# First attention of a two-layer block: values and ones in one product, maxima as rows of the queries, both kinds of scores interleaved over four row groups

## The chip, the cores and the metric

The kernel runs on one core of one Trainium2 chip. The metric is device time in microseconds, the median of three runs. A further execution was profiled; times of single instructions come from it. PE is the matmul engine, PEld its weight loads, DVE the vector engine, ACT the scalar (activation) engine, POOL the general SIMD engine, SP the engine whose queue issues the DMAs. SBUF is the on-chip memory, PSUM the eight banks that PE writes.

## The reference, cut to what matters

Two layers are computed one after the other. Each normalises its input, modulates it per sample, runs an attention-like part, adds the result to the input, and does the same with a feed-forward-like part. Only the first attention is touched by the change:

```python
# x: (16, 256, 128); sa, ca, ga: per-sample modulation, (16, 1, 128)
h = _layernorm(x, axis=-1) * (1 + ca) + sa
x = x + ga * _L0_attn_ref(h, Wq, bq, Wk, bk, Wv, bv, Wo, bo)

def _L0_attn_ref(hidden_states, Wq, bq, Wk, bk, Wv, bv, Wo, bo):
    HIDDEN, HEADS, HEAD_DIM = 128, 16, 8
    SCALE = HEAD_DIM ** (-0.5)
    b, s, d = hidden_states.shape
    q = (hidden_states @ Wq.T + bq).reshape(b, s, HEADS, HEAD_DIM)
    k = (hidden_states @ Wk.T + bk).reshape(b, s, HEADS, HEAD_DIM)
    v = (hidden_states @ Wv.T + bv).reshape(b, s, HEADS, HEAD_DIM)
    scores = jnp.einsum('bqhd,bkhd->bhqk', q * SCALE, k)
    probs = jax.nn.softmax(scores.astype(jnp.float32), axis=-1)
    out = jnp.einsum('bhqk,bkhd->bqhd', probs, v).reshape(b, s, d)
    return out @ Wo.T + bo
```

After it come a six-layer local transformer, a state-space layer and a low-rank linear layer. The change leaves their code as it is.

## The kernel before

`block_kernel` computes both modulations, then calls `full_attention`, `local_transformer` and `state_space`. The whole activation stays in SBUF, features on partitions (`c.xT`, 128 by 4096). `full_attention` (L132 to L425) is the first attention. Its unit of work is one sample (`u`, 16 of them, 256 tokens); two samples make a group (`g`, 8 of them). The 16 heads are numbered as four row groups `r` (32 partitions each) by four heads `j` within a row group, 8 features each.

**Per group**, `before` (a Python generator, L183) loads the tokens (`xin`), transposes them into `xT` (`px`), takes mean and variance on DVE (`a0st`, `a0mv`), the inverse root on POOL (`inv_sqrt`, L53), normalises on DVE (`xn`, L212), transposes to features (`to_features`, tile `ln`, result `hT`), and makes queries and keys. The query tile `qm` (L223) has four copies of the queries, one for each `j`; in copy `j` a per-partition scale `hm` zeroes all partitions but those of head `j`, so that 32 rows can be used where a head has only 8. Two copies are written by ACT (L226) and two by DVE (L231).

**Per sample**, `values` (L246) makes the value tile `vp`, in which each head has 8 columns of values and 32 of zeros; `turn` (L290) transposes the negated row maxima, as bfloat16 high and low parts made by POOL (L287, L288), into `nT`; `after` (L368) divides by the sums (`rT`, `oT`), multiplies by the output weights (`py`), and adds to `xT`.

**Per step** `k` (64 of them, four to a sample) three things happen. `scores(k, half)` (L263) computes scores with the queries on partitions, 128 queries of two heads `j` in the two row groups of that half, into two PSUM banks `s` (two buffers in all), and DVE takes the maxima (L283). `exponentials(k)` (L306) computes the same scores again with the keys on partitions, 128 keys by 2 heads by 256 queries, in all four row groups (L314, tile `sT`, four banks), adds the negated maxima by eight bfloat16 products with a selection matrix `selm` (L325), and ACT exponentiates (L336, tile `e`). `gather(k, j)` (L339) multiplies the exponentials by the values into `po[:, 0]` and by a tile of ones into `po[:, 1]`, in four column groups of 32 (L359); the first gather of a sample clears the bank with four bfloat16 products (`zb`, L347).

**The order** is written out by hand (`tc.manual_schedule()`, L395 to L425): every engine takes its instructions in the order in which this loop issues them. In step `k` come `exponentials(k)`, `scores(k + 5, 0)`, a slot, `gather(k - 1, 0)`, a slot, `scores(k + 5, 1)`, `gather(k - 1, 1)`, a slot. A slot runs the first pending generator up to its next `yield`. Pending ones are `before` of a later group (appended when `k % 8 == 3`), and, put in front of it, `values`, `turn` (one step before its sample's first exponentials) and `after`. So the first five steps have scores alone, and the last five exponentials and gathers alone. All of `px`, `ln`, `pq`, `pk`, `pv`, `pm`, `py` share one PSUM bank (tag `mm`, one buffer, L147): each waits until the reader of the one before it is done. In float32 every product shows as two records of PE and two weight loads.

Of the kernel before, what the change touches and what calls it, by code (L numbers as in the profile page):

```python
# [10 lines left out]
F32 = mybir.dt.float32  # L11
# [120 lines left out]
def full_attention(c, a, m):  # L132
# [4 lines left out]

    nc, tc = c.nc, c.tc
    HJ, R = 4, 32
    with ExitStack() as ctx:  # L140
# [8 lines left out]

        w4 = wp.tile([P, 4, D], F32, tag="w4", name="w4")  # L150
        for j, n in enumerate(("WqT", "WkT", "WvT", "WoT")):
            nc.sync.dma_start(w4[:, j, :], a[n])
        b3 = wp.tile([P, 3], F32, tag="b3", name="b3")
        nc.sync.dma_start(b3, a["b0"])
        bv = wp.tile([P, D], F32, tag="bv", name="bv")
        nc.sync.dma_start(bv, a["bv"].partition_broadcast(P))

        hm = wp.tile([P, HJ], F32, tag="hm", name="hm")
        nc.sync.dma_start(hm, a["c_head"])
# [3 lines left out]
        selm = wp.tile([P, HJ, P], BF16, tag="selm", name="selm")  # L163
        sel1 = wp.tile([P, HJ], F32, tag="sel1", name="sel1")
        nc.sync.dma_start(sel1, a["c_hmax"])
        nc.vector.tensor_copy(selm, sel1.unsqueeze(2).to_broadcast([P, HJ, P]))
        zb = wp.tile([P, R], BF16, tag="zb", name="zb")
        nc.gpsimd.memset(zb, 0.0)

        VB = R + HD0  # L170
        one = wp.tile([P, HJ * VB], F32, tag="one", name="one")
        nc.gpsimd.memset(one, 0.0)
        nc.gpsimd.memset(one.rearrange("p (h x) -> p h x", x=VB)[:, :, 0:HD0], 1.0)
        vp, nms = [], []
        for i in range(2):
            t = wp.tile([P, NT, H0 * VB], F32, tag=f"vp{i}", name=f"vp{i}")
            nc.gpsimd.memset(t, 0.0)
            vp.append(t)
            t = wp.tile([P, NT, HJ, R], BF16, tag=f"nm{i}", name=f"nm{i}")
            nc.gpsimd.memset(t, 0.0)  # L180
            nms.append(t)

        def before(g, q):  # L183
# [25 lines left out]
            yield  # L209
            xn = sb.tile([P, n, D], F32, tag="xn", name="xn")  # L210
            for i in range(n):
                nc.vector.tensor_scalar(  # L212
                    xn[:, i, :], xin[:, i, :], mv[:, i, 0:1], r[:, i : i + 1], ALU.subtract, ALU.mult
                )
                if i % 2:
                    yield
# [7 lines left out]
            for j in range(HJ):  # L224
                if j % 2 == 0:
                    nc.scalar.activation(  # L226
                        qm[:, :, j, :], pq, AF.Identity, bias=hb[:, j : j + 1], scale=hm[:, j : j + 1]
                    )
            for j in range(HJ):
                if j % 2:  # L230
                    nc.vector.tensor_scalar(  # L231
                        qm[:, :, j, :], pq, hm[:, j : j + 1], hb[:, j : j + 1], ALU.mult, ALU.add
                    )
            yield
            pk = ps.tile([P, GT], F32, tag="mm", name="pk")
            nc.tensor.matmul(pk, w4[:, 1, :], hTf, start=True, stop=True)
            kT = gp.tile([P, G, S], F32, tag="kT", name="kT")
            nc.scalar.activation(
                kT.rearrange("p b s -> p (b s)"), pk, AF.Identity, bias=b3[:, 1:2], scale=1.0
            )  # L240
# [3 lines left out]
        tops, rows_, sums, exps = {}, {}, {}, {}  # L244

        def values(u):  # L246
            g, b = divmod(u, G)
            v, hT = vp[b], made[g]["hT"]
            pv = ps.tile([P, NT, D], F32, tag="mm", name="pv")
            for t in range(NT):  # L250
                nc.tensor.matmul(
                    pv[:, t, :], hT[:, b, t * P : (t + 1) * P], w4[:, 2, :], start=True, stop=True
                )
            for t in range(NT):
                nc.vector.tensor_tensor(
                    v[:, t, :].rearrange("p (h x) -> p h x", x=VB)[:, :, 0:HD0],
                    pv[:, t, :].rearrange("p (h x) -> p h x", x=HD0),
                    bv.rearrange("p (h x) -> p h x", x=HD0),
                    ALU.add,
                )  # L260
            yield

        def scores(k, half):  # L263
# [5 lines left out]
            if i == 0 and half == 0:  # L269
                tops[u] = sb.tile([P, NT, HJ, HJ], F32, tag="mx", name="mx")  # L270
            ss = [sp.tile([P, 2, S], F32, tag="s", name="s") for _ in range(2)]
            for j in range(2):
                for r, s in enumerate(ss, 2 * half):
                    rows = slice(r * R, (r + 1) * R)
                    nc.tensor.matmul(  # L275
                        s[:, j, :],
                        qm[rows, b, jj + j, t * P : (t + 1) * P],
                        kT[rows, b, :],
                        start=True,
                        stop=True,  # L280
                    )
            for r, s in enumerate(ss, 2 * half):
                nc.vector.tensor_reduce(tops[u][:, t, r, jj : jj + 2], s, AX.X, ALU.max, negate=True)  # L283
            if i == 3 and half == 1:
                nm = nms[b]
                hi, lo = nm[:, :, :, 0:HJ], nm[:, :, :, HJ : 2 * HJ]
                nc.gpsimd.tensor_copy(hi, tops[u])  # L287
                nc.gpsimd.tensor_tensor(lo, tops.pop(u), hi, ALU.subtract)  # L288

        def turn(u):  # L290

            nm = nms[u % G]
            pm = ps.tile([P, NT, P], F32, tag="mm", name="pm")
            for t in range(NT):
                nc.tensor.matmul(
                    pm[:, t, :],
                    nm[:, t].rearrange("p r x -> p (r x)"),
                    c.identb,
# [3 lines left out]
            rows_[u] = sb.tile([P, S], BF16, tag="nT", name="nT")  # L302
            nc.vector.tensor_copy(rows_[u], pm.rearrange("p t x -> p (t x)"))
            yield

        def exponentials(k):  # L306
            u, i = divmod(k, 4)
            g, b = divmod(u, G)
            jj, kt = 2 * (i // 2), i % 2
            qm, kT, nT = made[g]["qm"], made[g]["kT"], rows_[u]  # L310
            ss = [tp.tile([P, 2, S], F32, tag="sT", name="sT") for _ in range(HJ)]
            for r, s in enumerate(ss):
                rows = slice(r * R, (r + 1) * R)
                nc.tensor.matmul(  # L314
                    s,
                    kT[rows, b, kt * P : (kt + 1) * P],
                    qm[rows, b, jj : jj + 2, :],
                    start=True,
                    stop=True,
                    skip_group_check=True,  # L320
                )
            for j in range(2):
                for r, s in enumerate(ss):
                    rows = slice(r * R, (r + 1) * R)
                    nc.tensor.matmul(  # L325
                        s[:, j, :],
                        selm[rows, jj + j, :],
                        nT[rows, :],
                        start=False,
                        stop=True,  # L330
                        skip_group_check=True,
                    )
            exps[k] = []
            for s in ss:
# [1122 lines left out]
```

## Time and profile before

| what | value |
| --- | --- |
| median of 3 runs | 4379.85 us (4375.7 to 4380.5) |
| the profiled execution: time, span | 4380.97 us, 4379.2 us (so 1.8 us lie outside the span) |
| busy over the span: PE, PEld, DVE, ACT, POOL | 95%, 57%, 80%, 57%, 58% |
| first scores (L275) start | 29.0 us |
| first exponentials' products (L314) start | about 63 us |
| last step with scores ends | 438.0 us |
| last gather ends | about 458.7 us |
| two samples in the middle, one group made beside them (224.53 to 276.03) | 51.50 us: PE 49.23, DVE 31.17, ACT 20.15, POOL 3.39 busy |
| one sample near the end, no group made (379.03 to 402.52) | 23.49 us: PE 23.30, DVE 13.57, ACT 8.26, POOL 1.18 busy |

How to read it: the first attention is the stretch from about 17 us, where its weights are loaded, to about 463 us, some 10% of the span. In the views quoted below a row of the table by stages gives, after the stretch and its length, each engine's busy time and instruction count, then the clock that PE was granted (1.00 is full speed, 0.50 half), the share of the DMA engines and GB/s. A row of the timeline gives start, duration, engine, line, operation, tiles written and read, shapes, how many instructions were merged, and in brackets how long the engine sat idle before and for whom. A busy PE is not PE at its peak: its records overlap, so the distance from one start to the next tells more than a duration.

### The profile page before, as it was taken

How to read it: one execution, taken by the hardware profiler on the slowest of the kernel's cores; microseconds unless marked ns; L12 is line 12 of the kernel's file. 1: busy time of each engine (PE TensorE's matmuls, PEld its weight loads, DVE VectorE, ACT ScalarE, POOL GpSimd, SP SyncE). 2: the span in 40 equal slices, each digit the busy share in tenths (PEclk: the TensorE clock that was granted, in tenths of full speed). 3: DMA queues.
4: the chain of work that ended last, by engine and by line, in shares of the span. 5: the costliest groups of instructions: out<-in, count | busy, mean ns of one | idle time of the engine just before them, and what ended most of it. 6: DMA issues, size and time to landing. Idle time of an engine off the chain costs nothing. (4 is left out here: it accounts for less than half of the span.)

```text
span 4379.2 us, 100775 instructions
## 1 busy us (share of the span) xinstructions
PE 4146.0 (95%) x43950; PEld 2479.5 (57%) x43950; DVE 3521.1 (80%) x4992; ACT 2483.0 (57%) x3219; POOL 2530.8 (58%) x1532
## 2 busy tenths in 40 slices
PE   7999599999999999999999999999999999779998
PEld 4455355565665655656556565565665655445554
DVE  4665588888888888888888888888888988459997
ACT  2333455555555555555555555555555555379995
POOL 0000366656666666666666666666666666258887
PEclk9999799999999999999999999999999999889999
DMA  0000100000000000000000000000000000033433
GB/s 23 6 4 1 54 2 1 2 2 22 7 2 2 2 22 6 2 2 2 22 6 2 1 2 22 6 2 1 2 2 2 2 1 2 13 97 105 114 104 85
DMA packets 58773, 82.86 MB, mean 19 GB/s; under 512 B 5256, under 2 KB 30428, under 8 KB 57564
## 3 DMA queue, kind: packets, MB, share of 16 engines
q1 hardware_dynamic: 58332, 76.41, 6.3%
q8 instruction: 346, 5.67, 0.5%
q14 instruction: 95, 0.78, 0.1%
HBM read 73.78 MB, written 2.62 MB: 17 GB/s over the span
## 5 line engine op out<-in xcount | busy, mean ns | idle before, releaser
L594 POOL TENSOR_TENSOR u<-u,w 128x1024 f32<-128x1024 f32 x384 | 902.0, 2360 | 323.9 <-DVE w L577 183.6
L608 POOL TENSOR_TENSOR u<-u,r 128x1024 f32<-128x1024 f32 x384 | 720.3, 1902 | 176.3 <-DVE r L604 176.3
L561 ACT ACTIVATE sq<-pq 128x1024 f32<-128x1024 f32 x384 | 388.5, 1024 | 665.1 <-PE pq L554 331.1
L554 PE MATMUL pq<-wqk,F 128*128 128x512 f32 x1536 | 723.0, 598 | 4.0 <-ACT sq L561 1.4
L694 POOL TENSOR_TENSOR pp<-pp,sm 128x1024 f32<-128x1024 f32 x192 | 367.1, 1912 | 619.9 <-DVE sm L690 619.9
L731 PE MATMUL py<-at,wvo 128*128 128x256 f32 x3072 | 714.4, 383 | 2.3 <-ACT at L722 2.3
L712 PE MATMUL pa<-pT,xw 32*128 32x512 f32 x3072 | 653.4, 617 | 30.3 <-ACT sq L561 29.3
L731 PEld LDWEIGHTS py<-at,wvo 128*128 128x128 f32 x3072 | 570.4, 191 | 134.9 <-issue 47.9
L566 DVE TENSOR_TENSOR u<-pq,cosl 128x1024 f32<-128x1024 f32 x384 | 463.3, 1207 | 190.4 <-ACT sq L561 190.4
L577 DVE TENSOR_TENSOR w<-pq,sinl 128x512 f32<-128x512 f32 x768 | 491.3, 681 | 82.9 <-PE pq L554 82.5
L722 ACT COPY at<-pa 128x1024 f32<-128x1024 f32 x384 | 383.6, 1012 | 277.0 <-PE pa L712 274.1
L588 DVE TENSOR_REDUCE ss<-sq 128x16 f32<-128x1024 f32 x384 | 455.8, 1198 | 2.6 <-ACT sq L561 1.1
L554 PEld LDWEIGHTS pq<-wqk,F 128*128 128x128 f32 x1536 | 273.8, 191 | 275.7 <-issue 244.1
L617 PEld LDWEIGHTS pt<-ident,u 128*128 128x128 f32 x3072 | 350.0, 142 | 123.9 <-issue 73.2
L617 PE MATMUL pt<-ident,u 128*128 128x128 f32 x3072 | 400.0, 276 | 20.0 <-POOL u L608 19.6
L712 PEld LDWEIGHTS pa<-pT,xw 32*128 32x128 f32 x3072 | 234.1, 185 | 291.2 <-issue 182.7
L1219 DVE TENSOR_TENSOR_SCAN s<-da,db 128x512 f32<-128x512 f32 x256 | 301.4, 1208 | 25.8 <-PE db L1213 11.5
L795 PE MATMUL fp<-hT,w 128*128 128x512 f32 (+1 forms) x576 | 268.0, 602 | 39.8 <-DVE w L577 38.0
L657 PEld LDWEIGHTS s<-kT,qT 64*32 64x32 f32 x24576 | 254.4, 105 | 82.0 <-issue 81.0
L283 DVE TENSOR_REDUCE mx<-s 128x2 f32<-128x512 f32 x256 | 164.8, 686 | 152.2 <-PE s L275 150.3
L657 PE MATMUL s<-kT,qT 64*32 64x64 f32 x24576 | 285.5, 226 | 0.5 <-ACT kT L625 0.5
L1229 PE MATMUL y<-hc,ident 128*128 128x512 f32 x512 | 244.3, 604 | 16.0 <-POOL hc L1223 14.2
(214 smaller groups left out, 6199.5 us busy)
## 6 DMA issues: line engine op xcount, KB each, us to landing
btd<-bc SPq DMA_DIRECT2D x72, 512.0 KB, 5.3
bte<-bc SPq DMA_DIRECT2D x56, 256.0 KB, 5.2
wqk<-in_Wqk SPq DMA_DIRECT2D x6, 1024.0 KB, 7.8
wv<-in_LWvT SPq DMA_DIRECT2D x6, 512.0 KB, 5.3
wo<-in_Wo SPq DMA_DIRECT2D x6, 512.0 KB, 9.0
xin<-in_x SPq DMA_DIRECT2D x8, 256.0 KB, 2.9
out<-ot SPq DMA_DIRECT2D x8, 256.0 KB, 6.2
w<-in_W SPq DMA_DIRECT2D x6, 341.0 KB, 2.9
```

The costliest lines, as they stand in the source:

```text
L554: nc.tensor.matmul(q.p[:, x], self.F[:, g.b0 + b, o : o + P], g.l.wqk[:, k, x, :], start=True, stop=True)
L561: self.c.nc.scalar.activation(q.sq, q.p, AF.Square)
L566: self.c.nc.vector.tensor_tensor(q.u.rearrange("p h x d -> p x h d"), q.p, g.l.cosl[:, t, k].unsqueeze(2).to_broadcast([P, 2, HEADS, DH // ...
L577: self.c.nc.vector.tensor_tensor(q.w[:, :, x], q.p[:, 1 - x], g.l.sinl[:, t, k, x, :].unsqueeze(1).to_broadcast([P, HEADS, DH // 2]), ALU. ...
L588: self.c.nc.vector.tensor_reduce(g.ss[b][:, t, k, :], q.sq.rearrange("p x h d -> p h x d"), AX.XY, ALU.add)
L594: self.c.nc.gpsimd.tensor_tensor(q.u, q.u, q.w, ALU.add)
L608: self.c.nc.gpsimd.tensor_tensor(uf, uf, g.r[b][:, t, k, :].unsqueeze(2).to_broadcast([P, HEADS, DH]), ALU.mult)
L617: self.c.nc.tensor.transpose(q.pt[:, j, :], uf[:, j * P : (j + 1) * P], self.c.ident)
L657: nc.tensor.matmul(s[qs, e, j, :], qT[es, j, qs], kT[es, j, ks : ks + 2 * W], start=False, stop=True, skip_group_check=True,)
L712: self.c.nc.tensor.matmul(pa[:, x, :], g.xw[b, t][qs, k, :], g.pT[b, t][qs, k, :], start=(k == 0), stop=(k == 1),)
L722: self.c.nc.scalar.copy(self.at[:, :, o : o + 2 * W].rearrange("p h (w q) -> p w h q", q=W), g.pa[b, t, i].rearrange("p w (h q) -> p w h q ...
L731: self.c.nc.tensor.matmul(g.py[b], g.l.wvo[:, h, :], self.at[:, h, :], start=(h == 0), stop=(h == HEADS - 1),)
```

## The change

Six things are done at once in `full_attention`.

1. The maxima are no longer added by separate products. They are turned in float32 (`pm`, 16 partitions), copied by ACT, and written by four DMAs per sample (one for each `j`) into a partition of each row group of `qm` that copy `j` leaves at zero (`TOP`: 24, 25, 0, 1). The keys get a second version with ones on those partitions (`kT[:, v]`, two ACT instructions per group instead of one).
2. Each head's values and ones lie side by side in `vp`, so that one product yields both output and sum; heads `j` 0 and 1 write `po[:, 0]`, heads 2 and 3 `po[:, 1]`. In `after`, `swap` products bring each sum beside its output (`pr`), and the output product is two with halved weights (`wo`). The value bias moves into the output bias (`bo`, `bg`).
3. `pair(k, h)` interleaves: two row groups compute the scores of step `k + 6`, the other two the transposed scores of step `k`, in the order first head `j` of the scores, exponents, second head `j`.
4. Work changes engines: `xn` from DVE to POOL, `vp`, `nT`, `yg` from DVE to ACT, one of four `qm` copies from DVE to ACT, the division from DVE to POOL, with a new copy `o` of the sums by ACT before it.
5. `AHEAD` goes from 5 to 6; `before` starts at `k % 8 == 2`, `turn` at `k % 4 == 2`, ahead of `values`; the `yield`s move.
6. The loads at the start are in another order, with four new constants.

```diff
-        def exponentials(k):
+        def exponents(k, h):
+            u, i = divmod(k, 4)
+            g, b = divmod(u, G)
+            jj, kt = 2 * (i // 2), i % 2
+            qm, kT = made[g]["qm"], made[g]["kT"]
+            ss = []
+            for r in range(2 * h, 2 * h + 2):
+                rows = slice(r * R, (r + 1) * R)
+                s = tp.tile([P, 2, S], F32, tag="sT", name="sT")
+                nc.tensor.matmul(s, kT[rows, jj // 2, b, kt * P : (kt + 1) * P],
+                    qm[rows, b, jj : jj + 2, :], start=True, stop=True)
+                ss.append((r, s))
+            return ss
+        def exponentials(k, ss):
+            for r, s in ss:
+                e = pp.tile([P, 2, S], F32, tag="e", name="e")
+                nc.scalar.activation(e, s, AF.Exp)
+                exps[k, r] = e
+        def pair(k, h):
+            first, second = k + AHEAD < N, 0 <= k < N
+            if first:
+                scores(k + AHEAD, h, 0)
+            if second:
+                ss = exponents(k, 1 - h)
+            if first:
+                scores(k + AHEAD, h, 1)
+                maxima(k + AHEAD, h)
+            if second:
+                exponentials(k, ss)
         def turn(u):
-            nm = nms[u % G]
-            pm = ps.tile([P, NT, P], F32, tag="mm", name="pm")
...
-            rows_[u] = sb.tile([P, S], BF16, tag="nT", name="nT")
-            nc.vector.tensor_copy(rows_[u], pm.rearrange("p t x -> p (t x)"))
+            top = tops.pop(u)
+            pm = ps.tile([HJ * HJ, NT, P], F32, tag="mm", name="pm")
+            for t in range(NT):
+                nc.tensor.matmul(pm[:, t, :], top[:, t].rearrange("p j r -> p (j r)"), c.ident, ...)
+            nT = sb.tile([HJ * HJ, S], F32, tag="nT", name="nT")
+            nc.scalar.copy(nT, pm.rearrange("p t x -> p (t x)"))
+            rows = made[g]["qm"].rearrange("(r x) b j s -> x r b j s", x=R)
+            for j in range(HJ):
+                nc.sync.dma_start(rows[TOP[j]][:, b, j, :], nT[j * HJ : (j + 1) * HJ, :])
         def gather(k, j):
-            for x in range(2):
-                for r, e in enumerate(exps[k]):
-                    w = vp[b][:, kt, o : o + R] if x == 0 else one[...]
-                    nc.tensor.matmul(sums[u][r * R : (r + 1) * R, x, :], w, e[:, j, :], ...)
+            for r in range(HJ):
+                nc.tensor.matmul(sums[u][r * R : (r + 1) * R, jj // 2, :],
+                    vp[b][:, kt * HJ + r, (jj + j) * R : (jj + j + 1) * R], exps[k, r][:, j, :], ...)
         def after(u):
-            nc.vector.reciprocal(rT, po[:, 1, :])
-            nc.vector.tensor_tensor(oT, po[:, 0, :], rT, ALU.mult)
-            yield
-            nc.tensor.matmul(py, w4[:, 3, :], oT, start=True, stop=True)
-            nc.vector.tensor_scalar(yg, py, b3[:, 2:3], m[:, 2, u : u + 1], ALU.add, ALU.mult)
+            o = sb.tile([P, 2, S], F32, tag="o", name="o")
+            nc.scalar.copy(o, sums.pop(u))
+            yield
+            for x in range(2):
+                nc.tensor.matmul(pr, swap[:, x, :], o[:, x, :], start=(x == 0), stop=(x == 1))
+            nc.vector.reciprocal(rT, pr)
+            nc.gpsimd.tensor_tensor(o, o, rT.unsqueeze(1).to_broadcast([P, 2, S]), ALU.mult)
+            yield
+            yield
+            for x in range(2):
+                nc.tensor.matmul(py, wo[:, x, :], o[:, x, :], start=(x == 0), stop=(x == 1))
+            nc.scalar.activation(yg, py, AF.Identity, bias=bg[:, u : u + 1], scale=m[:, 2, u : u + 1])
         def values(u):
-            for t in range(NT):
-                nc.vector.tensor_tensor(v[:, t, :]..., pv[:, t, :]..., bv..., ALU.add)
+            nc.scalar.copy(v..., pv...)
         def before(g, q):
                 nc.vector.bn_aggr(mv[:, i, :], st[:, i, :])
             inv_sqrt(c, r, r, [P, n])
-            yield
             for i in range(n):
-                nc.vector.tensor_scalar(xn[:, i, :], ...)
-                if i % 2:
-                    yield
+                nc.gpsimd.tensor_scalar(xn[:, i, :], ...)
+            yield
+            yield
             to_features(c, ps, xn, m, 0, 1, g, hT)
-        AHEAD, N = 5, 4 * B
+        AHEAD, N = 6, 4 * B
-                if k % 8 == 3 and (k // 8 + 2) * G < B:
+                if k % 8 == 2 and (k // 8 + 2) * G < B:
-                if k % 4 == 3 and 0 <= k + 1 < N:
-                    todo.insert(0, turn((k + 1) // 4))
                 if k % 4 == 2 and 0 <= k + 2 < N:
                     todo.insert(0, values((k + 2) // 4))
-                if 0 <= k < N:
-                    exponentials(k)
-                if k + AHEAD < N:
-                    scores(k + AHEAD, 0)
+                    todo.insert(0, turn((k + 2) // 4))
+                pair(k, 0)
                 slot()
                 if 0 < k <= N:
                     gather(k - 1, 0)
                 slot()
-                if k + AHEAD < N:
-                    scores(k + AHEAD, 1)
+                pair(k, 1)
                 if 0 < k <= N:
                     gather(k - 1, 1)
```

## The prediction

> **What bounds the kernel now.** I read the table by stages first, then the groups of the stage, then its timeline. Only the first attention changes, about 29 to 459 us. Two samples in mid-stage, and a late one without a group made beside it, read:
>
> ```profile
> 224.53:276.03 51.50, 49.23 (x552) 25.97 (x556) 31.17 (x60) 20.15 (x38) 3.39 (x7) 1.00 0.02 7
> 379.03:402.52 23.49, 23.30 (x272) 12.56 (x276) 13.57 (x22) 8.26 (x16) 1.18 (x3) 1.00 0.01 2
> ```
>
> PE is busy 96 to 99%. It is the bound, but a second loop lies close behind it:
>
> ```profile
> 271.43 1.03 PE L275 MATMUL s<-kT,qm 32*128 32x256 f32 x8
> ...
> 272.39 0.64 PE L359 MATMUL po<-e,vp 128*32 128x256 f32 x8
> ...
> 272.49 1.29 DVE L283 TENSOR_REDUCE mx<-s 128x2 f32<-128x512 f32 x2 [2.22 <-PE s L275]
> ...
> 273.39 1.57 PE L275 MATMUL s<-kT,qm 32*128 32x256 f32 x8
> ...
> 274.58 1.29 DVE L283 TENSOR_REDUCE mx<-s 128x2 f32<-128x512 f32 x2 [0.80 <-PE s L275]
> 274.89 0.64 PE L359 MATMUL po<-e,vp 128*32 128x256 f32 x8
> ...
> 275.89 1.14 PE L314 MATMUL sT<-qm,kT 32*128 32x512 f32 x8
> ```
>
> Starts give PE's prices: half a step's scores 0.96 (271.43 to 272.39), a gather 1.00 (274.89 to 275.89), and from the same timeline four exponents' products 0.96 and their eight bfloat16 products 0.22. A step is 0.96 + 0.22 + 2x0.96 + 2x1.00 = 5.10, a sample 20.4 and its slots 3.1.
> The loop: `s` has two banks, so scores wait for the maxima before (273.39, first bank; 273.83, second) and the maxima wait for the scores. Maxima follow maxima after **2.09** (272.49 to 274.58): 1.29 reducing, 0.80 waiting. Where both banks start together (280.12) the maxima begin 1.17 later (281.29), against 0.75 after the second bank where the first started 0.44 ahead; the loop is then 1.17 + 1.29 + 0.05 = 2.51. Neither `nT` nor exponentials slow this down: ACT idles before them, waiting for PE.
>
> **The change on PE.** The eight bfloat16 products go (0.22), gathers halve (1.00 to 0.57: half the 0.86 of stream, 0.14 of change-over kept), and the four exponents run beside the scores (0.96 saved). A pair with its change-over costs 1.07, with gather 1.64; a step 3.28 instead of 5.10. Over 59 steps that is 107 us of PE work, the most there is to win. That row groups run side by side, not in issue order, is seen where the first exponents begin:
>
> ```profile
> 62.45 1.32 PE L275 MATMUL s<-kT,qm 32*128 32x256 f32 x2
> ...
> 63.00 1.23 PE L314 MATMUL sT<-qm,kT 32*128 32x512 f32 x2
> ...
> 63.04 1.58 PE L275 MATMUL s<-kT,qm 32*128 32x256 f32 x5
> ```
>
> Five records of scores issued before the exponents start after them. [...]
>
> **But 1.64 is under 2.09: the loop of DVE becomes the bound**, two per step, 4.18. And PE's 0.45 of slack is just the head start that makes 2.09 rather than 2.51, so most slot work shows. Interval a runs from a step's first pair to its second, b to the next step. Prices from rows: `pv` 0.64, `px`, `ln` 0.6, `pq`, `pk` 1.06, `zb` 0.23, `py` and `pr` 1.06 each (0.63 for today's half, plus 0.43 of stream), exponentials end 2.28 after a pair starts (0.53 to the second pass, 0.59 for it, 0.08 to ACT, 1.08 for two).
> - k mod 4 = 2, a: `pm`, then `pv`, which needs its bank. ACT copies `nT` only behind the exponentials: 2.28 + 0.45 = 2.75, `pv` to 3.44. **3.44**; b 2.51.
> - 3 and 0: four of 2.09.
> - 1, a: `pr`, `zb`: 1.07 + 1.06 + 0.23 + 0.57 = **2.93**. b: reciprocal 1.76 from 2.35 to 4.1, POOL's multiply 1.32 (a 128x512 product at L1223) to 5.5, `py` 1.06: **3.68**.
>
> A sample is 20.9, today 23.49. A group made beside two samples adds: `px` and its late load 0.4, statistics 0.5; `pk` waits for the bank of `pq`, whose readers now are three ACT copies of 0.7 behind the exponentials (2.33 to 4.55), then runs to 5.65, +3.56 on 2.09; after it 2.51 instead of 2.09. Two samples: 46.7, today 51.50.
>
> **Unseen costs.** `pm` in float32: 0.22 (today's) to 0.64 (`pv`); I take 0.45. ACT's copy of 16x256: 0.19 (128x64, L1120) to 0.56 (128x256, L123); 0.45. The multiply: 0.95 (half of L608's 1.90) to 1.32; the upper, for equal shape. Together -14 to +5 us over 16 samples. POOL's `xn`: 0.37 (128x64, L597) to twice that, four times; two slots cover them, and uncovered each would delay `ln`. DMAs: 64 more on SP, 0.43 each to issue, 1.6 (`bc`) to 2.9 (`xin`) to land: the two needed first are in at 2.75 + 0.86 + 1.6..2.9 = 5.2..6.5, needed at 10.1 (3.44 + 2.51 + 2x2.09): hidden. Queued behind them on SP is only the next `xin`. The bf16 casts on POOL go from beside other work: nothing. `vp` and `yg` on ACT lie in its idle time; so do two `kT` copies.
>
> **Sum.** First scores at 29.0 as now (the loads' order and `pb` move this by -1 to +1.4). Before the first exponentials PE runs at half pace:
>
> ```profile
> 31.14 1.29 DVE L283 TENSOR_REDUCE mx<-s 128x2 f32<-128x512 f32 x2 [5.03 <-PE s L275]
> ...
> 31.89 2.67 PE L275 MATMUL s<-kT,qm 32*128 32x256 f32 x8 [0.78 <-DVE mx L283]
> 33.99 1.29 DVE L283 TENSOR_REDUCE mx<-s 128x2 f32<-128x512 f32 x2 [1.56 <-PE s L275]
> ```
>
> A half costs 2.85; today ten halves and 5.5 of slots make 34. Twelve make 34.2, and slots 8 (`pq` waits for `hT`, `pk` for `qm`): exponentials start at 71, today 63. 58 steps: 8.4 for the first two, 6 for the low clock at their start, 6x46.7, 2x20.9, 337 in all, to 408; today 375 for 59. The last six steps without scores: 6x3.28, 1.8 for `pv`, 3.3 for `py`, 1.2 for the last gather, 26, today 20.7. Last gather at 434, today 458.7: -25. The last sample's tail is longer by copy, `pr`, multiply and half of `py` (3 us), half covered by the next stage's normalisation, already running then: +1.5. So 4380.97 - 23.5 = 4357.5 for the profiled execution; against the median, 1.1 lower, **4357**.
>
> **Rivals.**
> 1. *The clock stays down* (slower). The granted clock is half at 464 to 504 us and full again only after dense work, and in the prologue the pace is half though PE looks busy:
>
> ```profile
> 32.00:36.00 4.00, 4.00 (x14) 2.82 (x16) 1.72 (x3) 0.36 (x1) 0.00 (x0) 1.00 0.00 2
> ```
>
> (The 1.00 is from before the first clock record; the products' pace is the measure.) Two row groups of four are in use there; full pace comes at 72 us, once all four and the gathers fill PE. [...] So what counts seems to be how much of the array works, and the change leaves PE more idle: `pk`'s stall is 1.9 us. At half pace an interval is 3.05 (pair 1.95, gather 1.05), slots 10 a sample: 34.5, against 23.4 on average. +11 a sample; from 2.1 cold samples on the gain is gone. Six would give **4423**. For it: warming today takes exponents, bfloat16 products and full gathers. Against: at half pace PE is the bound again, hence dense. Chance 0.17.
> 2. *The rows stored in `qm` hold back scores, or pairs run in order.* If scores of the group's other sample wait for the four DMAs, eight samples wait till 6.5 rather than 3.44: +25, **4382**. If a pair does not overlap as it says, nine of sixteen intervals lose their head start of 0.44: +29, **4386**. For: all are in one tile. Against: the rows at 63 us, and the parts written and read differ. Chance 0.20, a fifth of it slower by over 0.2%.
> 3. *The stalls hide.* Without the waits for ACT and POOL the a of 2 is 2.73, the b of 1 2.70, the `pk` interval 3.76: 1.7 a sample and 1.9 a group, -36, **4321**. For: ACT is idle two thirds of the time. Against: its queue is in order. Chance 0.19.
>
> **How the numbers follow.** The forecast has 0.44 (4343 to 4371 by the unseen costs and the start). Measurement tells 0.2%, about 9 us, from no change. Faster: 0.44 + 0.19 = 0.63; same: 0.16, four fifths of rival 2; slower: 0.17 + 0.04 = 0.21. The range goes from below rival 3 to the milder part of rival 1, two cold samples over no gain: 4315 to 4400.
>
> **What would show it.** Maxima 2.09 to 2.5 apart with DVE, not PE, behind the waits; PE under 85% busy; waits of `pv` for `nT`, `pk` for `qm`, `py` for `o`; a sample of about 21, with a group 23.4; first exponentials near 71 us. Wrong if the granted clock falls in the stage, if scores wait for a DMA, or if intervals without slot work differ from 2.09.

## The result, and the profile after

The changed kernel takes **4390.79 us** (median of 9 runs, 4385.3 to 4394.5), the kernel before 4379.2 us beside it (9 runs, 4375.4 to 4380.9). The ratio is 1.0028, 95% interval 1.0018 to 1.0039: slower by 0.28%, where 4357 was forecast. The profiled execution took 4388.87 us, its span 4386.8 us.

The busy shares would not show it: PE falls from 95% to 94%, DVE from 80% to 79%. The marks of the stage do:

| mark (us from the span's start) | before | forecast | after |
| --- | --- | --- | --- |
| first scores | 29.0 | 29.0 | 35.5 |
| first exponents' products (their pair starts at 79.3 after) | 63.0 | 71 | 80.0 |
| last gather ends | 458.7 | 434 | 473.0 |
| from there to the end of the span | 3920.5 | +1.5 | 3913.8 |

So the stage itself loses 14.3 us, and the layers behind it give 6.6 us back. Two samples with a group made beside them, one late sample without, and the stretch before the first exponents (columns as in the table by stages before):

```profile
214.42:265.68 51.26, 43.65 (x380) 22.77 (x376) 25.90 (x46) 25.73 (x48) 8.12 (x9) 0.97 0.02 7
...
396.57:419.53 22.96, 20.02 (x188) 10.58 (x184) 11.92 (x19) 10.33 (x20) 1.99 (x2) 1.00 0.00 1
...
35.50:80.00 44.50, 38.00 (x119) 22.47 (x119) 17.44 (x34) 7.83 (x12) 4.16 (x5) 1.00 0.00 1
```

PE's busy time in the late sample fell from 23.30 to 20.02 and DVE's from 13.57 to 11.92, as the change intends, yet the sample lasts 22.96 where it lasted 23.49. Neither engine fills it: each waits for the other. The timeline of one plain interval, in which no slot adds work to PE, says for what:

```profile
208.02 1.29 DVE L296 TENSOR_REDUCE mx<-s 128x2 f32<-128x512 f32 x2 [0.60 <-PE sT L324]
...
208.77 1.08 PE L282 MATMUL s<-kT,qm 32*128 32x256 f32 x3 [0.27 <-DVE mx L296]
...
209.37 0.18 PEld L282 LDWEIGHTS s<-kT,qm 32*128 32x128 f32 x1 [0.30 <-DVE mx L296]
...
209.38 0.70 PE L324 MATMUL sT<-qm,kT 32*128 32x512 f32 x2
...
209.39 0.89 PE L282 MATMUL s<-kT,qm 32*128 32x256 f32 x4
...
209.91 0.59 PE L324 MATMUL sT<-qm,kT 32*128 32x512 f32 x2
...
210.53 1.08 ACT L337 ACTIVATE e<-sT 128x512 f32<-128x512 f32 x2 [1.51 <-PE sT L324]
210.62 1.29 DVE L296 TENSOR_REDUCE mx<-s 128x2 f32<-128x512 f32 x2 [0.82 <-PE sT L324]
```

Maxima follow maxima after **2.60** (208.02 to 210.62), not 2.09. At 208.77 the first bank's first score starts; the second bank is free at 209.37, and the exponents issued behind its score begin right after (209.38). The first bank's second score starts at 209.39, its last pass at 209.71, and its record ends at 210.08. The maxima that read it begin at 210.62, which is 0.12 after the records of the exponents end (209.91 + 0.59 = 210.50). They are named as the releaser: `sT L324`, which the maxima do not read.

What the maxima and PE waited for between 80 and 473 us (total, times, longest), two answers of the waits view:

```profile
DVE mx L296 <- PE sT L324: 170.0, 102, 4.0
```

```profile
PE s L282 <- DVE mx L296: 17.1, 56, 0.9
PE py L395 <- POOL o L390: 16.0, 15, 1.1
PE pk L247 <- DVE qm L242: 14.9, 6, 2.5
PE pv L263 <- ACT nT L308: 6.4, 15, 0.4
```

`pk` waits 2.5 us once in a group. The timeline there:

```profile
225.54 1.12 PE L235 MATMUL pq<-hT,w 128*128 128x512 f32 x2
...
226.71 2.12 ACT L238 ACTIVATE qm<-pq,hb,hm 128x512 f32<-128x512 f32 x3
228.86 0.81 DVE L242 TENSOR_SCALAR qm<-pq,hm,hb 128x512 f32<-128x512 f32 x1 [1.84 <-ACT qm L238]
...
229.72 1.79 PE L247 MATMUL pk<-hT,w 128*128 128x512 f32 x2 [2.49 <-DVE qm L242]
231.44 0.80 PE L282 MATMUL s<-kT,qm 32*128 32x256 f32 x2
```

DVE's copy of `qm` runs behind ACT's three, not beside them, and `pk` then takes 1.79, where `pq`, of the same form, took 1.12: the granted clock is at half. It is so for 3.4 us once in each of the six groups (128, 179, 230, 281, 332, 384 us), which the profile before does not have inside the stage. That DVE's copies come behind ACT's was already so before, when each engine made two of them (the groups of the kernel before from 0 to 450 us, with the idle time and its releaser at the end):

```profile
L231 DVE TENSOR_SCALAR qm<-pq,hm,hb 128x512 f32<-128x512 f32 x16 | 12.2, 806 | 19.6 <-ACT qm L226 19.6
```

And at the start PE waits for a load (total, times, longest, up to 36 us):

```profile
PE pb L180 <- DMA bvc<-in_bv: 7.3, 1, 7.3
```

`pb`, the new product for the value bias, stands in PE's order ahead of `px` of the first group, which starts at 23.4 instead of 7.1.

### The profile page after: what moved, and what is told of

Read it like the earlier page. It is cut to its first block, busy times and chain, and to the rows that moved or that the text cites. A ratio compares the mean times of both kernels' runs of the same rounds, so it can differ in the third digit from the quotient of the medians.

```text
span 4386.8 us, 97989 instructions
## 1 busy us (share of the span) xinstructions
PE 4104.9 (94%) x42544; PEld 2447.8 (56%) x42544; DVE 3481.1 (79%) x4876; ACT 2527.3 (58%) x3299; POOL 2568.6 (59%) x1552
## 4 chain that ended last, share of the span: by engine, by line
PE 57%; DVE 24%; ACT 4%; issue 2%; POOL 1%; SPq 0%; ACTq 0%; DVEq 0%; POOLq 0%; DMA 0%
PE pq L566 13%; PE py L743 11%; PE pa L724 10%; DVE w L589 4%; DVE u L578 4%; PE fp L807 4%; ACT sq L573 3%; PE fy L829 3%; PE s L669 3%; PE pt L629 3%; PE y L1241 3%; DVE ss L600 3%; PE db L1225 2%; DVE s L1231 2%; DVE pp L687 1%
## 5 line engine op out<-in xcount | busy, mean ns | idle before, releaser
L724 PE MATMUL pa<-pT,xw 32*128 32x512 f32 x3072 | 651.6, 616 | 30.3 <-ACT sq L573 29.2
L629 PE MATMUL pt<-ident,u 128*128 128x128 f32 x3072 | 398.2, 275 | 20.5 <-POOL u L620 19.7
L1241 PE MATMUL y<-hc,ident 128*128 128x512 f32 x512 | 244.2, 604 | 16.1 <-POOL hc L1235 14.3
```

The source lines that it names most:

```text
L629: self.c.nc.tensor.transpose(q.pt[:, j, :], uf[:, j * P : (j + 1) * P], self.c.ident)
L724: self.c.nc.tensor.matmul(pa[:, x, :], g.xw[b, t][qs, k, :], g.pT[b, t][qs, k, :], start=(k == 0), stop=(k == 1),)
```

## The experiments

Three losses to separate: the interval of 2.60, `pk` with the clock, and the start. All ratios are to the kernel before, with 95% intervals.

**Exponents behind the scores.**

```diff
             if first:
                 scores(k + AHEAD, h, 0)
-            if second:
-                ss = exponents(k, 1 - h)
-            if first:
                 scores(k + AHEAD, h, 1)
                 maxima(k + AHEAD, h)
             if second:
-                exponentials(k, ss)
+                exponentials(k, exponents(k, 1 - h))
```

> Edit to the changed kernel: in a pair both heads' score products are issued before the exponents' products, nothing else. Theory A (the maxima wait for PE's completion count, which by issue order includes the exponents' products, whose second pass ends 0.5 us after the scores): maxima follow maxima after 2.1 us instead of 2.60 in plain intervals, a sample without a group 22.96 -> about 20.9, two samples with one 51.2 -> about 47, time 4390.8 -> about 4360. Theory B (four row groups at once make the score products themselves slower): no interval moves by more than 0.1 us, time within 5 us of 4390.8.

Measured: 4373.8 us, ratio 0.9989 (0.9980 to 0.9998). Plain intervals are 2.09, a late sample 20.81, the last gather ends at 449.2, 23.8 us sooner. A plain interval of this kernel:

```profile
394.24 1.29 DVE L296 TENSOR_REDUCE mx<-s 128x2 f32<-128x512 f32 x2 [0.87 <-PE s L282]
...
395.08 0.99 PE L282 MATMUL s<-kT,qm 32*128 32x256 f32 x3
...
395.61 0.69 PE L324 MATMUL sT<-qm,kT 32*128 32x512 f32 x1
395.61 0.46 PE L282 MATMUL s<-kT,qm 32*128 32x256 f32 x1
...
396.14 0.60 PE L324 MATMUL sT<-qm,kT 32*128 32x512 f32 x2
396.33 0.69 DVE L296 TENSOR_REDUCE mx<-s 128x2 f32<-128x512 f32 x1 [0.80 <-PE s L282]
```

What runs beside what is nearly the same as in the changed kernel: the second bank's score starts at 395.59, the exponents and the first bank's second score together at 395.61. But the maxima begin 0.75 after 395.59, while the exponents still run (to 396.74); in the changed kernel it was 1.25 after 209.37. Only the order of issue differs. So it isn't the sharing of the array that held the maxima; they waited for products issued ahead of their own. Nor was it the second bank's last score, whose record also ends at 210.50 in the changed kernel: here that record ends at 396.71, after the maxima have begun. The gain in time is 17 us where about 30 was expected: the groups still bring `pk`'s wait and the half clock (25.4 to 28.1 us for a sample beside a group), and the layers behind took 9 us more than in the changed kernel (3922.8 against 3913.8), which the edit does not touch.

**Exponents ahead of both scores.** The same three lines, moved to the top of `pair`.

> The changed kernel, only the place of the exponents moved: ahead of both scores of the pair instead of between them. Theory (maxima wait for a count of finished products that goes in the order of issue, so every exponent issued ahead of the last score is waited for): the plain interval stays at 2.6 or grows, since the exponents still stand ahead; last gather at 473 or later, time 4385 to 4400. Rival (the place between the two scores of a half is what holds the second score back): the plain interval comes back to 2.09 to 2.2, last gather near 450, time near 4370.

Measured: 4370.58 us, ratio 0.9981 (0.9971 to 0.9991); plain intervals 2.09 to 2.15, last gather at 451.9. This expectation of the theory was wrong, and the rival's numbers came. The timeline says which of the two reasons holds:

```profile
394.75 1.29 DVE L296 TENSOR_REDUCE mx<-s 128x2 f32<-128x512 f32 x2 [0.80 <-PE s L282]
...
395.63 0.70 PE L324 MATMUL sT<-qm,kT 32*128 32x512 f32 x2
...
395.64 0.94 PE L282 MATMUL s<-kT,qm 32*128 32x256 f32 x3
...
396.17 0.59 PE L324 MATMUL sT<-qm,kT 32*128 32x512 f32 x2
...
396.91 1.29 DVE L296 TENSOR_REDUCE mx<-s 128x2 f32<-128x512 f32 x2 [0.86 <-PE s L282]
```

I had overlooked when the exponents start. Issued ahead of every score, they begin with the first bank (395.63) and not behind the score that waits for the second bank (396.10). They end at 396.76, and the last pass of the first bank's scores at 396.80: waiting for them costs nothing. The rival needs a score that is held back by the exponents between; the rows of the changed kernel show none (209.39, 0.02 after the second bank's). So, by these three runs (2.60, 2.09, 2.09 to 2.15), the loss takes two things together: exponents issued ahead of a score are waited for, and they themselves stand behind a score that waits for its bank.

**Not interleaved**, all four exponents of a step at the start of `pair(k, 0)`, then the scores by halves:

```diff
+            if second and h == 0:
+                exponentials(k, exponents(k, 0) + exponents(k, 1))
             if first:
                 scores(k + AHEAD, h, 0)
-            if second:
-                ss = exponents(k, 1 - h)
-            if first:
                 scores(k + AHEAD, h, 1)
                 maxima(k + AHEAD, h)
-            if second:
-                exponentials(k, ss)
```

> Edit to the changed kernel: all four exponents' products of a step at the start of its first pair, then the scores of each half by themselves, as before the change. PE's work grows by 0.96 us a step. Theory A: first interval 0.96 + 1.07 + 0.57 = 2.6, second 2.09, sum 4.7 against 5.2 now, so about -20 us (4370), and about 10 us slower than with scores first. Theory B: the same sum here, but faster than with scores first by 20 us or more, since only here are the row groups apart. If interleaving is worth what it removes from PE (0.96 a step), this run is slower than 4390.8 by up to 56 us.

Measured: 4414.46 us, ratio 1.0084 (1.0069 to 1.0099), 44 us over the 4370 that was expected. A late sample takes 23.24, which is near the changed kernel's; but samples with a group take 27.7 to 35.9, with half clock for 55 us inside the stage, two stretches of it 20.5 us long (at 130 and 400). Whether the order or the clock cost it was open.

**`pk` a slot later**: one more `yield` between `pq` and `pk`.

> Edit to the changed kernel: one more yield between the query product and the key product, so that pk comes one slot later. Theory A': PE's stall of about 3 us for the bank of pq, and the 3.4 us at half clock that follow it in each of six groups, both go: 7.3 us in that interval -> 2.7, with a later pk costing 1, so 3.5 to 4.5 us a group, 4390.8 -> about 4366; no clock of 0.50 in the records between 90 and 470 us. Rival: the stall only stands beside DVE's work and the clock falls for another reason: time within 5 us, six half-clock windows remain.

Measured: 4369.81 us, ratio 0.9983 (0.9973 to 0.9993). The window that is two samples in the changed kernel:

```profile
214.42:265.68 51.26, 45.61 (x412) 24.68 (x411) 27.14 (x47) 28.08 (x54) 8.14 (x9) 1.00 0.02 7
```

The granted clock is 1.00 instead of 0.97, and more products fit in; two samples take 47.2 instead of 51.3. Between 92 and 454 us no stretch of half clock is left, and the last gather ends at 449.3. Plain intervals stay at 2.60, so this loss is separate from the first.

**Not interleaved, and `pk` a slot later.**

> The changed kernel, not interleaved (the four exponents of a step together at its start, then scores by halves), and pk one slot later. Open from the run without interleaving alone: whether its 4414 came from the order or from the clock, which stood at half for 57 us of its stage. Theory (clock): pk's stall let the clock fall there, so with pk later the stretches go and two samples take 23.3 + 24.5 instead of 51 to 59; last gather at 455 to 460, time 4377 to 4382; the order itself then costs 0.3 a sample against the changed kernel. Rival (the order itself keeps the array too empty): stretches of half clock stay, time over 4400.

Measured: 4380.08 us, ratio 1.0005 (0.9996 to 1.0015). The stretches of half clock are gone (none between 99 and 454 us) and two samples take 23.3 + 26.1. So 34 us of the 4414 came from `pk`'s wait and the clock that fell with it, not from the order. The group costs 1.6 more than expected (26.1 against 24.5), and the last gather ends at 462.4, where 455 to 460 was expected. Against the changed kernel with the same repair (4369.81), interleaving as the change does it is worth 10 us.

**`pb` behind the first group**: `pb`, `bo` and `bg` moved behind the first group's `before`.

> Edit to the changed kernel: the product for the output bias (pb) and its two vector operations are issued after the first group is made. Theory: px and ln of the first group stand behind pb on PE, which waits for the eighth load; without it the first scores start at 29 us instead of 35.5 and all later marks move by the same 6.5: 4390.8 -> 4384. Rival: the first scores wait for the loads (hm, WqT) or for three query copies on ACT as long: under 2 us.

Measured: 4386.1 us, ratio 1.0020 (1.0011 to 1.0029); first scores at 30.3 instead of 35.5, last gather at 465.5, 7.5 sooner; one of the six half-clock stretches is missing too.

**The three repairs together.**

> The changed kernel with three repairs together: the exponents of a pair issued behind both scores and the maxima, pk one slot later, pb behind the first group. Theory: the losses add, since each has its own place. With the exponents behind the scores the plain interval is 2.09 again and a sample 20.8 (so measured alone); with pk a slot later a group adds about 1.3 instead of 4 to 7 to a sample, so two samples take 43 to 44 and no half-clock stretch falls inside the stage; without pb the first scores are at 30.3. From the run with the exponents behind (last gather at 449.2): less 6 x 4 and less 5, that is about 420. The layer behind took 3913.8 to 3923.7 in the runs so far, so the time is 420 + 3922 + 2 = 4344, range 4335 to 4356. Rival: the loop that gets faster leaves PE still less to do, and the clock falls again; every group with a stretch of 6.8 us at half clock would give 3 to 4 us a group back, 4365 to 4370.

Measured: **4348.18 us**, ratio 0.9931 (0.9919 to 0.9944). The last gather ends at 426.1, the median is 42.6 us under the changed kernel's. Alone the repairs moved the last gather by 23.8, 23.7 and 7.5 us, 55.0 in sum, together by 46.8, so in the stage they do not quite add; it ends 6 us later than expected, and two samples take 45.0 instead of 43 to 44. The time is 4 us over the expected 4344, as the layers behind took 3919.7, 2 us less than was assumed. Two samples with a group, and a late one:

```profile
219.03:264.01 44.98, 40.71 (x376) 22.06 (x372) 26.09 (x45) 25.49 (x48) 8.13 (x9) 1.00 0.03 8
374.84:395.64 20.80, 19.21 (x184) 10.67 (x180) 12.07 (x17) 10.33 (x20) 1.99 (x2) 1.00 0.01 3
```

**`pv` and `py` a slot later besides**: a `yield` more before each, two empty ones of the loading fewer.

> The three repairs, and besides pv and py one slot later each (a yield more before each, two empty yields of the loading fewer). Theory (the third rival of the prediction, tried on the mended loop): of a sample's 20.8, 8 intervals of 2.09 are 16.7, and most of the other 4.1 is PE waiting, for nT before pv and for o before py; a slot later both are ready. By the prediction's prices that is 0.7 for pv and 1.0 for py in a sample, 27 us in sixteen samples. Last gather 20 to 27 us before that of the kernel with three repairs, time 4317 to 4326. Rival: the slots' own work on PE (pr, py, pv) is what makes the intervals long, not the waits; then less than 8 us are gained and the intervals only change places.

Measured: 4338.49 us, ratio 0.9904 (0.9889 to 0.9919). The waits of `py` for `o` (0.9 each) and of `pv` for `nT` (0.5 each) are gone, a late sample is 19.55, samples beside groups are 1.1 shorter on average. The last gather comes 8.4 us sooner, not 20 to 27: the waits are 1.4 a sample where 1.7 were priced, and two stretches of half clock (101 and 125 us, 6.8 each) appeared beside the first group, whose two samples take 26.6 and 26.5 instead of 22.2 and 23.2. The rival's number, less than 8, came nearer than the theory's, but its reason did not hold: the waits did make the intervals long, and they are gone.

**Half of each maximum left out**: the three repairs, the reduction over the first 128 of 256 keys.

```diff
-                nc.vector.tensor_reduce(tops[u][:, t, jj : jj + 2, r], s, AX.X, ...)
+                nc.vector.tensor_reduce(tops[u][:, t, jj : jj + 2, r], s[:, :, 0:P], AX.X, ...)
```

> The three repairs, with the maxima taken over the first 128 of the 256 keys only: half of each reduction is left out, so the maxima are not those of whole rows. Theory (the loop of scores and maxima bounds the stage): a reduction of 0.69 becomes about 0.42, the loop 0.75 + 0.33 + 0.42 + 0.05 = 1.55, which is under PE's 1.64; so plain intervals fall from 2.09 to 1.64 to 1.7. In a sample four to five of eight are plain, the others wait for pv, pr and py and gain at most 0.3; a sample 18.5 to 19.3 instead of 20.8, the last gather 24 to 35 us before 426, time 4313 to 4325. Rival (PE itself bounds it and maxima wait by chance): intervals stay above 2.0, less than 8 us are gained.

Measured: 4327.26 us, ratio 0.9881 (0.9866 to 0.9896). Plain intervals fall from 2.09 to 1.65, near the 1.64 that was priced for PE alone, a late sample from 20.81 to 19.18, the last gather by 21.7 us to 404.4. So the loop of scores and maxima did bound the mended kernel. The gain is a little under what was expected, since `py` and `pv` wait as before (13.6 and 6.8 us between 100 and 400 us).

**Products that compute nothing**, to keep the array in use before the first exponents, with the three repairs: first 15 of them, then 43. The shares of the array that the expectations name are estimates, worked out from the trace of the kernel before: rows times columns of each product over 128 x 128, by the time that it streams, summed over stretches of 3.4 us, the length of the shortest stretch in its clock records.

```diff
+        def warm(n):
+            d = tp.tile([P, 2, S], F32, tag="sT", name="warm")
+            for _ in range(n):
+                nc.tensor.matmul(d[:, 0, :], w4[:, 0, :], w4[:, 0:2, :]..., start=True, stop=True)
...
+                if k < 0:
+                    warm(1)
                 pair(k, 0)
```

> The three repairs, and besides products that compute nothing: three of 128x128 by 128x256 between pq and pk of the first group and one before every pair of the first six steps, into a bank of sT that nobody reads. Theory: before the first exponents TensorE stays at half pace because scores fill two of its four row groups, so that the array is busy by a quarter to a third, however busy PE looks; from the trace before, windows of 3.4 us with over about 0.86 of the array in use bring full pace, and over about 0.38 keep it. The three products make one dense window, the one for each half keeps 0.6. Then the first scores start about 2 us later than without (at about 32) and the first exponents come at 63 to 66 instead of 75, the full clock by about 30 instead of 86: 10 to 15 us less, 4329 to 4335 if the three repairs give 4344. Rival: only time, or only what the clock decides by itself, brings full pace; then the products cost their 12 x 1.8 us at half pace, less what lies in PE's idle time, 5 to 20 us more.

Measured: 4349.62 us, ratio 0.9930 (0.9918 to 0.9943), no gain over the three repairs. Full clock came at 24.4 us, right after `pq` and the first three products, fell at 31.2, came at 58.5, fell at 61.9 and came at 85.8. The stretches moved, but one product for each half was too few to hold it: by the same estimate 0.31 and 0.38 of the array were in use in the stretches of 3.4 us before the two falls.

> The three repairs with more of the products that compute nothing (128x128 by 128x256, 0.43 us at full pace): three between pq and pk of the first group, four behind pk, and six in each of the first six steps, two ahead of each pair and one ahead of the slots. In the run with twelve of them the full clock came at 24.4, after pq and the first three, and fell at 31.2, after a stretch in which PE waited for kT; it came and fell once more. Theory (what counts is the share of the array in use): now no window before the first exponents falls under 0.4, so the full clock comes at about 24 and stays; a step costs 6 x 0.43 + 2 x 0.96 = 4.5, six of them with 4 of slots 31, first exponents at 62 to 65 instead of 75.6; time 4348 less 10 to 14, 4334 to 4339. Rival (the clock does not follow the load of the array): stretches of half pace come as before, each of the 36 products then costs 0.85, and the first exponents come at 80 or later, time 4352 to 4360.

Measured: 4339.66 us, ratio 0.9910 (0.9895 to 0.9925). The full clock holds from 24.2 to 44.7 and from 54.9 on; it fell once, where PE waited for the second group's `ln` and `pq` (an estimated 0.34 of the array in use in the 3.4 us before). The first exponents come at 71.7 (75.6 without the products), the last gather at 417.2 (426.1). Expected was 62 to 65 and a clock that stays full, so the direction is right and the size was not: each half now costs 2.56 at full pace, because the products fill PE (busy for 16.95 of the 17.10 us from 54.9 on), and the second group's waits remain. At half and at full pace, the same eight records of scores:

```profile
53.95 1.58 PE L284 MATMUL s<-kT,qm 32*128 32x256 f32 x8
...
57.81 1.13 PE L284 MATMUL s<-kT,qm 32*128 32x256 f32 x8
```

The kernel with three repairs has in the same time:

```profile
54.90:72.00 17.10, 14.93 (x48) 8.29 (x45) 5.88 (x10) 3.46 (x5) 0.00 (x0) 1.00 0.00 1
72.00:86.50 14.50, 14.08 (x68) 8.55 (x68) 5.74 (x9) 3.26 (x6) 0.00 (x0) 1.00 0.01 1
```

(The 1.00 lies before its first clock record, at 86.5.) PE shows 87% and 97% busy there, at half pace all the while.

**All of it**: the three repairs, `pv` and `py` later, and the 43 products.

> The three repairs, pv and py a slot later, and the same products that compute nothing. If the gains add: 4338.5 less 10 to 14, that is 4325 to 4329. With pv and py later the run without these products had two stretches of 6.8 us at half clock, at 101 and 125, 3.5 us together; if a clock that is full from the start keeps them away too, 4321. Rival as in the kernel with the three repairs: no gain or 4 to 12 us more.

Measured: 4335.87 us, ratio 0.9903 (0.9886 to 0.9920), the fastest that computes the whole, though not apart from the run without the extra products (0.9904). The gains do not add: half clock comes back for 3.4 to 6.8 us at 42, 76, 96 and 120 us.

## Why the prediction was wrong

In the profiled execution the forecast was -23.5 us; it was +7.9. By its own steps:

- **The plain interval: the step that failed.** "two per step, 4.18" took the 2.09 of the kernel before, in which the maxima wait for their own scores. With exponents issued between the two heads, they wait for those too: 2.60. Four plain intervals in a sample make 2.04, and a late sample is 22.96 against 20.9 predicted, 2.06 more; over 14 samples that is 28.8, where the 58 steps (367.4 against 337) came out 30.4 us longer. Shown by moving the exponents: 2.09, 20.81 for the sample, and 23.8 us back at the last gather.
- **What starts show.** From rows I took it that products of different row groups start out of the order of issue. They do here too (exponents at 209.38, scores issued ahead of them and behind at 209.37 to 209.39, all at once). But the maxima began at 210.62, after the exponents ahead of the first bank's second score had ended (210.50), as if products were finished in order of issue; with the exponents issued behind they began 0.75 after the second bank's score and not 1.25. (The ends of records are modelled; when the maxima start is measured.) For pairs that do not overlap the second rival had +29; by the plain intervals it was 28.8 worse. That the sizes are so near is partly luck: the 29 was nine of sixteen intervals that lose a head start of 0.44, and it came as eight of sixteen that grow by 0.51. From starts I had concluded something on completion that starts don't show.
- **The start.** First scores at 29.0 were forecast, -1 to +1.4 for order of loads and `pb`. It was +6.5: I had priced `pb` as a product, and not what is queued behind it, the whole first group behind a load that lands at 22.5. Moving it gives 5.2 back.
- **Before the first exponents** 42 us were forecast, 43.8 it is. Half pace throughout, as said (`pq` takes 2.08 at 27.46, 1.12 at 225.54); the full clock comes at 90 (before: 72).
- **`pk`.** The interval was forecast at 5.65, taking DVE's copy of `qm` beside ACT's. It runs behind them (228.86, DVE idle before for ACT's last copy), as the row of the kernel before had shown for its own copies (19.6 us of waiting for ACT's); PE idles 2.5 us, the clock falls, and it is 7.34. Two samples then take 51.3; 4.1 of the 4.6 over forecast are the plain intervals, so against its own price `pk` costs only 0.5 a group more. Against a `pk` one slot later it costs 4.1 a group, 24 us in all. The three copies and the fourth read one tile, `pq`, and write one tile, `qm`, and the row has them follow each other (ACT's end at 228.83, DVE's starts at 228.86); why they do, no run here shows.
- **The last six steps**: 26 forecast, 26.2 measured. DMAs into `qm`: no wait of PE names one, as forecast. POOL's `xn` takes 0.79 each, over the bound of 0.74, and stays hidden. `pv`, `py` wait as forecast.
- **The layers behind**: +1.5 forecast, -6.6 measured. A stretch of half clock of 13.7 us in the first layer of the transformer, at 598 us before, is not there after. In the experiments this part took between 3912.9 and 3923.7 us, and over the fourteen traces it goes largely with the time that the clock stands at half behind the last gather: 121.6 us of it in the shortest (3912.9), 125.6 after, 152.9 before, 149.9 in the longest (3923.7). What sets these stretches was not settled; the prediction had no term for them.
- **The rivals.** The second came nearest in time (4386), and for a part of it ("pairs in order") in effect; but pairs do run side by side, and the head start of the first bank is in the rows and of no use. The first was right in small: one half-clock stretch per group, not six cold samples. The third, that stalls hide, did not come by itself; hidden on purpose they gave 1.1 to 1.3 a sample. Two of the prediction's own signs of being wrong are in the trace: the granted clock falls in the stage, and intervals without slot work are 2.60 apart, not 2.09.

What the change is worth with these losses taken out is shown by the three repairs: 31 us against the kernel before. The 107 us of PE's work that it removes could not all come, since DVE's loop of 2.09 lies close behind, as the prediction said, and half of a reduction taken away gave another 21.

## What to carry to other kernels

In the changed kernel the maxima waited as if PE's products were finished in order of issue: they followed each other after 2.60 with the exponents between the two scores, after 2.09 with the exponents behind, and after 2.09 to 2.15 with the exponents ahead of both, where the exponents start with the first bank (395.63). So issue what another engine waits for ahead of what nobody waits for yet, even where both run at once, and mind a product ahead that waits for a bank. When a bound moves from one engine to a loop of two, price the loop with the new instructions in the queue, not with the interval of the old one. And price a new instruction at the head of a queue by what it waits for, and count everything queued behind it.

## What was not expected of the hardware

- In the changed kernel products of different row groups start side by side (209.37 to 209.39), but the maxima began only after the exponents issued ahead of the first bank's second score had ended, by the modelled ends of the records (210.50, the maxima at 210.62): 1.25 us after the second bank's score instead of the 0.75 with the exponents issued behind, with nearly the same overlap on PE.
- In these traces the granted clock went with an estimate of how much of the array works, not with how long PE shows busy. In the kernel with three repairs PE was 87% busy from 54.9 to 72.0 us, with scores in two of four row groups, and 97% from 72.0 to 86.5, and stayed at half pace (its first clock record is at 86.5); in the dense run, with products over the whole array between them, the full clock came at 24 us and, after one fall at 44.7, held from 54.9 on. The estimate is the one described with the experiments. It counts 256 float32 columns as 0.21 us at full clock, half of the 0.43 between the starts of the two parts of a gather (279.16 and 279.59 in the kernel before), and as twice that at half clock (in the dense run three of the added products take 2.86 from 51.09 to 53.95 and 1.39 from 56.42 to 57.81). It can be taken over all fourteen traces, from the first full clock to the last gather: each of the 36 falls to half clock follows a stretch of 3.4 us with at most 0.39 of the array in use, and no stretch after which the clock stayed full has less than 0.37. In the changed kernel it is 0.18 to 0.21 before the six falls, and about 0.40 or more in every stretch after which the clock stayed full.
- The clock fell to half where PE waited 2.5 us for `pk`, and in the kernel that is not interleaved it stayed there for up to 20.5 us. Two samples of that kernel, one of them beside a group, then took 51 to 59 us, and 49 with `pk` later.
- Adding 43 products that compute nothing to the kernel with three repairs moved its last gather 8.9 us ahead.
